# A selective-scan block with experts on one core: the first scan group's products written straight into the result tile, the skip term added by a DMA of half the size

## The chip, the cores and the metric

The kernel runs on one core of a Trainium2 chip. The metric is the device time of one execution in microseconds, as the median of several runs. Five engines work side by side, each through its own list of instructions in order: TensorE (PE, with its weight loads as PEld), VectorE (DVE), ScalarE (ACT), GpSimd (POOL) and SyncE (SP, which here only issues transfers). POOL issues transfers too: those that add into their destination.

## The reference, cut to what matters

The input `x` is 16 samples of 256 positions with 256 features. Each sample is normalised; two branches are computed from the normalised sample and added to `x`.

```python
xn = layernorm(x)
# branch 1, per sample: E = 512 features, N = 16 states
hidden, gate = split(einsum('blh,he->bel', xn, W_in))
hidden = silu(causal_conv4(hidden) + conv_bias)
dt, Bm, Cm = split(hidden^T @ W_x, [128, 144])
dts = softplus(dt @ W_dt + b_dt)
dA  = exp(dts * A);  dBu = dts * Bm * hidden
state_t = dA_t * state_(t-1) + dBu_t            # scan over positions
scan_out = sum over the 16 states of state * Cm
y = (scan_out + hidden * D) * silu(gate)        # hidden * D is the skip term
branch1 = y^T @ W_out
# branch 2: 32 experts of width 96, the 8 best per position
branch2 = sum_e weight_e * (silu(xn @ w_gate_e) * (xn @ w_up_e)) @ w_down_e
out = x + branch1 + branch2
```

Everything is float32.

## The kernel before, in words

The work of one sample `b` is a set of small steps, each of one engine (the functions named below). They are not written in order. A planner (`Plan`, L20) is given for each step its engine, an assumed length, the steps it needs, the buffers it takes and gives back, and a due time: a base for the sample (`ORIGIN`, `PERIOD`, `RATE`) plus an offset for the kind of step (`DUE`, with `FIRST` and `LAST` for the first and last sample). It plays the engines through, always starting the ready step that is due first and prefers, by `STAY`, a step that needs no new activation table on ACT. The order that comes out is the order of the program. So a change of one step's length, needs or due time can move the steps of every engine, also of samples far apart. Buffers come in rings (`RINGS`): the n-th taker of a ring of size k waits until the (n-k)-th has been given back.

The scan branch of a sample:

- `load_x` (SP) loads `xt`; `stats`, `root`, `invert` give mean and deviation; `norm` (L366, ACT) writes the normalised sample into `xn`; `turn` (PE) transposes it into PSUM and `keep_turned` (ACT) copies it to `xnT`.
- `project` (PE, two halves, into PSUM banks "g" and "u"), `conv_first` (ACT) and `conv_rest` (DVE, twelve operations, L540) and `activate` (ACT) make `hs`. `params` (PE, `px`), `keep_params`, `send_params`, `widen`, `steps` make `dts`. `inputs` (L605, POOL) multiplies `dts` into `hs`, in place.
- The 16 states are taken in 8 groups `g` of two, and the four chunks of 128 features in two halves `u`; so there are 16 units per sample, each of two chunks. `fetch` (SP) brings the two B and C rows of a group to all partitions (`rep`). `feed` (POOL, L629) makes `bu` for a unit. `decay` (ACT, L643), `scan` (DVE, L651) and `read` (DVE, L661) run once per chunk; `read` multiplies the states with C and writes the products to `pr`, a ring of four.
- The sum over groups is made by transfers that add: `collect` (L664, issued by POOL) adds the 128 x 1024 products of a unit to `y[b, u]`. A `y` tile has two slots for the two states of a group. Before the first `collect` of a sample, `skip` (L594, ACT, one per chunk) has written hidden * D into slot 0 and `clear` (L601, POOL) zeros into slot 1. Collects of one `y` tile wait for each other's landing.
- After the last group `fold` (POOL, L685) adds the two slots, `gated` (POOL, L710) multiplies with the gate from `gate` (PE) and `gate_silu` (ACT), and `project_out` (PE, L720, `po`) multiplies with W_out. In the last sample DVE does the last collects and the gating.

The expert branch: `route` (PE, `pl`), `largest`, `expo`, `choose` (ten small DVE operations, L404 to L434) select and weigh the experts; `send_weights` writes the weights to DRAM (four transfers) and `spread` brings them to all partitions (`wr`, six transfers for a quarter). `gates` and `ups` (PE, L473, `pg` and `pu`), `silu` (ACT), `weigh` (POOL, L492), `combine` (DVE, L496, `h`) and `down` (PE, L508, `acc`) run over 12 pairs of chunks per sample.

The end of a sample: `load_again` (SP) loads `x` once more into `o`, `settle` and `finish` (DVE) add `acc` and `po` to it, and `store` (SP) writes it out. `o` is a ring of two.

At the start SP also loads all the weights: the experts' weights in four parts.

Of the kernel before, what the change touches and what calls it, by code (L numbers as in the profile page):

```python
# [11 lines left out]
F32 = mybir.dt.float32  # L12
AF = mybir.ActivationFunctionType
ALU = mybir.AluOpType
# [5 lines left out]
class Plan:  # L20
# [10 lines left out]
    STAY = -18.3  # L31
# [89 lines left out]
def mamba_moe_kernel(  # L121
# [30 lines left out]
    nc = tc.nc  # L152
# [26 lines left out]
    ORIGIN = -1.8  # L179
    PERIOD = 79.7  # L180
    RATE = 80.2

    DUE = dict(
        load_x=-146.0, stats=-45.5, root=-39.5, invert=-189.5, norm=235.5, turn=-297.0,
        keep_turned=-116.5, route=-81.5, largest=-193.5, expo=-102.5, choose=-538.5,
        send_weights=-21.0, project=-77.5, conv_first=328.0, conv_rest=265.5, activate=-374.5,
        params=-132.0, keep_params=-109.5, send_params=-242.0, widen=-104.5, steps=-17.0,
        skip=149.0, clear=-5.5, inputs=-96.5, fetch=-122.5, feed=168.5, decay=-16.5, scan=322.5,
        read=-130.1, collect=-20.0, spread=42.0, gates=-33.5, ups=238.5, silu=300.0, weigh=-19.5,
        combine=-120.0, down=26.5, settle=-222.0, gate=49.5, gate_silu=-159.0, fold=129.0,  # L190
        gated=378.5, project_out=-121.5, load_again=8.0, finish=-12.5,
    )
    EARLY = dict(
        load_x=171.0, load_experts=55.0, stats=31.0, turn=155.0, route=63.0, project=243.0,
# [3 lines left out]
        route=-144.0, largest=-26.0, expo=57.5, choose=266.0, project=309.5, conv_first=-246.5,  # L198
        conv_rest=-160.5, activate=289.0, params=-357.5, keep_params=261.5, widen=-38.5,
        steps=574.5, skip=-263.0, clear=-16.0, inputs=125.0, fetch=4.0, feed=-148.5, decay=-125.5,  # L200
        scan=-243.0, read=-43.0, collect=-97.5, spread=-33.5, gates=-12.5, ups=-178.5, silu=-161.0,
        weigh=288.0, combine=344.0, down=57.0,
# [3 lines left out]
        fetch=5.5, feed=-85.5, decay=55.5, scan=369.0, read=-177.5, collect=-114.5, spread=-3.5,  # L206
        gates=372.0, ups=44.5, silu=146.0, weigh=51.0, combine=141.5, down=275.5, settle=-6.0,
        gate=-31.5, gate_silu=-75.5, fold=-120.5, gated=412.0, project_out=-172.0, finish=299.5,
    )
    LEAD = -9.2  # L210
# [13 lines left out]
        xt=1, mv=1, st=1, std=1, xn=1, xnT=3, nmax=1, rest=1, dt=1, hs=2, dts=2, y0=2, y1=2,  # L224
        rep=3, bu=3, pr=4, da=AHEAD, g=2, u=2, acc=1, wr=2, sg=3, h=2, gs=2, o=2,
# [140 lines left out]
    def norm(b):  # L366
        xt = live["xt", b]
        rstd, nmr = live.pop(("st", b))
        xn = p1.tile([P, SPS, H], F32, tag="xn", name=f"xn_{b}")
        for s in range(SPS):  # L370
            nc.scalar.activation(
                xn[:, s, :], xt[:, s, :], AF.Identity, bias=nmr[:, s, :], scale=rstd[:, s, :]
            )
        live["xn", b] = xn

    def turn(b):
        xn = live.pop(("xn", b))
        pt = bank(f"pt_{b}", "u")
        for hc in range(HC):
            for s in range(SPS):  # L380
                nc.tensor.transpose(pt[:, ts(hc * SPS + s, P)], xn[:, s, ts(hc, P)], ident)
        live["pt", b] = pt
# [211 lines left out]
    def skip(b, c):  # L594
        hs = live["hs", b]
        u, j = divmod(c, CPU)
        if j == 0:
            live["y", b, u] = take(sb, f"y{u}", [P, CPU, NG, L], f"y_{b}_{u}")
        nc.scalar.activation(live["y", b, u][:, j, 0, :], hs[:, c, :], AF.Copy, scale=dsk[:, c, :])

    def clear(b):  # L601
        for u in range(PAIRED):
            nc.gpsimd.memset(live["y", b, u][:, :, 1, :], 0.0)
# [52 lines left out]
    def read(m):  # L656
        k, j = divmod(m, CPU)
        b, g, u = unit(k)
        if j == 0:
            live["pr", k] = take(sb, "pr", [P, CPU, NG, L], f"pr_{b}_{g}_{u}")  # L660
        nc.vector.tensor_mul(live["pr", k][:, j], live.pop(("da", m)), live["rep", b, g][:, 1])  # L661
# [86 lines left out]
    def add(kind, key, engine, length, due, *args, early=None, **kw):  # L748
# [15 lines left out]
        clear=clear, fold=fold, send_params=send_params, send_weights=send_weights, collect=collect, decay=decay, scan=scan, read=read,  # L764
# [17 lines left out]
    for b in range(B):  # L782
# [11 lines left out]
        add("norm", (b,), "ACT", 1.09, t, b, needs=[("invert", b)], takes=[("xn", ("xn", b))],  # L794
            gives=[x, ("rs", b)])
        xT = ("xnT", b)
        add("turn", (b,), "PE", 1.0, t, b, needs=[("norm", b)], gives=[("xn", b)],
# [33 lines left out]
        for c in range(EC):  # L831
            u, j = divmod(c, CPU)
            add("skip", (b, c), "ACT", 0.42, t, b, c,
                needs=[("activate", b)] + ([("skip", b, c - 1)] if j else []),
                takes=[] if j else [(f"y{u}", ("y", b, u))], gives=[hs])
        add("clear", (b,), "POOL", 0.93, t, b, needs=[("skip", b, c) for c in range(EC)])
# [7 lines left out]
        for r in range(UNITS):  # L844
# [5 lines left out]
            for j in range(CPU):  # L850
# [8 lines left out]
                    takes=[] if j else [("pr", ("pr", k))], gives=[("da", m), ("rep", b, g)])  # L859
            reads = [("read", CPU * k + j) for j in range(CPU)]  # L860
            if b == B - 1 and g == GROUPS - 1:
                add("collect", (k,), "DVE", 1.25, at + PERIOD / SLOTS, k, fn=collect_last,
                    needs=reads + [("fold", b, u)], gives=[("pr", k)])
                continue
            add("collect", (k,), "POOL", 0.61, at + PERIOD / SLOTS, k,
                needs=reads + [("clear", b)] + ([("collect", k - PAIRED)] if g else []),
# [88 lines left out]
```

## Time and profile before

| | us |
|---|---|
| median of 3 runs (1335.29 to 1336.34) | 1335.97 |
| the profiled execution, its own time | 1333.77 |
| its span, first to last instruction | 1332.0 |
| PE busy (97% of the span) | 1290.4 |
| POOL busy (89%) | 1189.2 |
| DVE busy (88%) | 1174.2 |
| ACT busy (86%) | 1142.6 |

The profile's times are those of one execution; a span is a little shorter than the time of the execution, and the sums below are made against the profiled execution. Rows of an engine name the source line, the operation and the tiles (result, then sources). The bracket behind a timeline row is the time for which the engine stood idle ahead of it, with the work whose end released it. One matmul step of the program is eight instructions of PE in such a row ("x8"), since a float32 matmul runs as two. The busy time of POOL contains time in which an operation is listed while the issue of a transfer ahead of it still holds the engine, so POOL's own cost is better read from one start to the next.

### The profile page before, as it was taken

How to read it: one execution, taken by the hardware profiler on the slowest of the kernel's cores; microseconds unless marked ns; L12 is line 12 of the kernel's file. 1: busy time of each engine (PE TensorE's matmuls, PEld its weight loads, DVE VectorE, ACT ScalarE, POOL GpSimd, SP SyncE). 2: the span in 40 equal slices, each digit the busy share in tenths (PEclk: the TensorE clock that was granted, in tenths of full speed). 3: DMA queues.
4: the chain of work that ended last, by engine and by line, in shares of the span. 5: the costliest groups of instructions: out<-in, count | busy, mean ns of one | idle time of the engine just before them, and what ended most of it. 6: DMA issues, size and time to landing. Idle time of an engine off the chain costs nothing.

```text
span 1332.0 us, 18939 instructions
## 1 busy us (share of the span) xinstructions
PE 1290.4 (97%) x5968; PEld 1109.9 (83%) x5968; DVE 1174.2 (88%) x1735; ACT 1142.6 (86%) x1904; POOL 1189.2 (89%) x835
## 2 busy tenths in 40 slices
PE   8979989999999999999999999999999999999998
PEld 6858778888888888888888888888888888888777
DVE  3878998989899898988989899798989989899896
ACT  5878698898989979799897988979899898987873
POOL 1769989999898999989899998999999999899995
PEclk9989999999999999999999999999999999999999
DMA  9999899899999899999999999989998998989994
GB/s 250 260 227 216 190 234 213 188 216 206 213 201 214 203 206 218 191 216 204 204 218 191 215 207 207 216 194 216 199 224 187 210 230 194 212 200 221 209 213 94
DMA packets 169941, 277.19 MB, mean 208 GB/s; under 512 B 37840, under 2 KB 103920, under 8 KB 169840
## 3 DMA queue, kind: packets, MB, share of 16 engines
q0 software_dynamic: 36576, 133.19, 53.1%
q1 hardware_dynamic: 130624, 142.75, 38.5%
q8 instruction: 47, 0.77, 0.2%
q10 hardware_dynamic: 2640, 0.05, 0.1%
q14 instruction: 54, 0.44, 0.1%
HBM read 137.51 MB, written 5.24 MB: 107 GB/s over the span
## 4 chain that ended last, share of the span: by engine, by line
PE 44%; DVE 17%; POOL 13%; issue 9%; DMA 8%; ACT 8%; SPq 1%; ACTq 0%; POOLq 0%; DVEq 0%
PE acc L508 11%; PE pg L473 10%; PE pu L473 10%; DVE da L651 6%; DMA rep<-bcd 5%; POOL bu L629 5%; POOL sg L492 5%; PE po L720 4%; PE px L555 4%; DVE hs L540 4%; DVE pr L661 4%; ACT da L643 3%; POOL y L666 2%; DMA y<-pr 2%; PE ph L519 2%
## 5 line engine op out<-in xcount | busy, mean ns | idle before, releaser
L629 POOL TENSOR_TENSOR bu<-rep,hs 128x1024 f32<-128x1024 f32 x256 | 726.7, 2942 | 73.3 <-DVE da L651 34.7
L651 DVE TENSOR_TENSOR_SCAN da<-da,bu 128x512 f32<-128x512 f32 x512 | 607.3, 1216 | 36.0 <-ACT da L643 26.0
L643 ACT ACTIVATE da<-dts,a_sb 128x256 f32<-128x256 f32 x1024 | 470.6, 473 | 90.9 <-DVE pr L661 68.9
L473 PE MATMUL pu<-xnT,wu_sb 128*128 128x256 f32 x1536 | 360.0, 381 | 12.3 <-DVE h L496 12.0
L508 PE MATMUL acc<-wd_sb,h 128*128 128x256 f32 x1536 | 363.4, 380 | 0.3 <-DVE o L732 0.3
L666 POOL DMA_DIRECT2D y<-pr x254 | 349.1, 1378 | 14.5 <-DVE h L496 5.2
L473 PE MATMUL pg<-xnT,wg_sb 128*128 128x256 f32 x1536 | 352.0, 383 | 9.2 <-ACT sg L486 7.0
L661 DVE TENSOR_TENSOR pr<-da,rep 128x512 f32<-128x512 f32 x512 | 336.1, 676 | 3.2 <-issue 1.6
L473 PEld LDWEIGHTS pu<-xnT,wu_sb 128*128 128x128 f32 x1536 | 292.3, 191 | 54.8 <-DVE h L496 14.4
L473 PEld LDWEIGHTS pg<-xnT,wg_sb 128*128 128x128 f32 x1536 | 294.5, 192 | 51.4 <-ACT sg L486 8.2
L508 PEld LDWEIGHTS acc<-wd_sb,h 128*128 128x128 f32 x1536 | 291.6, 191 | 39.9 <-DVE o L732 0.6
L492 POOL TENSOR_TENSOR sg<-sg,wr 128x512 f32<-128x512 f32 x192 | 295.6, 1793 | 32.4 <-ACT rstd L353 24.9
L496 DVE TENSOR_TENSOR h<-pu,sg 128x512 f32<-128x512 f32 x192 | 131.3, 684 | 81.7 <-POOL sg L492 39.9
L643 ACT ACT_TABLE_LOAD x154 | 197.6, 1283 | 2.8
L486 ACT ACT_TABLE_LOAD x81 | 103.9, 1283 | 1.5
L486 ACT ACTIVATE sg<-pg 128x512 f32<-128x512 f32 x192 | 104.0, 593 | 0.9
L540 DVE SCALAR_TENSOR_TENSOR hs<-ph,small,hs 128x255 f32<-128x255 f32 (+2 forms) x192 | 90.2, 478 | 5.3 <-ACT hs L531 0.7
L710 POOL TENSOR_TENSOR y<-y,gs 128x512 f32<-128x512 f32 x30 | 73.8, 2893 | 0.1
L685 POOL TENSOR_TENSOR y<-y 128x512 f32<-128x512 f32 x32 | 71.3, 2230 | 0.0
L720 PE MATMUL po<-wout_sb,y 128*128 128x256 f32 x256 | 61.6, 384 | 9.9 <-DVE hs L540 7.8
L720 PEld LDWEIGHTS po<-wout_sb,y 128*128 128x128 f32 x256 | 47.4, 190 | 21.0 <-POOL y L710 7.8
L555 PE MATMUL px<-hs,wx_sb 128*32 128x256 f32 (+1 forms) x256 | 61.4, 387 | 2.4 <-ACT sg L486 2.4
(64 smaller groups left out, 804.3 us busy)
## 6 DMA issues: line engine op xcount, KB each, us to landing
y<-pr POOLq DMA_DIRECT2D x254, 512.0 KB, 7.0
rep<-bcd SPq DMA_DIRECT2D x128, 512.0 KB, 6.4
wr<-wd SPq DMA_DIRECT2D x128, 192.0 KB, 6.2
wr<-wd SPq DMA_DIRECT2D x128, 128.0 KB, 6.1
wr<-wd SPq DMA_DIRECT2D x128, 64.0 KB, 5.7
xt<-L_attn_input_states_dram SPq DMA_DIRECT2D x16, 256.0 KB, 6.9
o<-L_attn_input_states_dram SPq DMA_DIRECT2D x16, 256.0 KB, 6.0
out_dram<-o SPq DMA_DIRECT2D x16, 256.0 KB, 5.2
```

What stands on the lines that cost most here:

```text
L473: nc.tensor.matmul(p[:, j, :], w[:, hc, ts(c, P)], xs[:, hc, :], start=(hc == 0), stop=(hc == HC - 1),)
L486: nc.scalar.activation(sg, live.pop(("g", b, q)), AF.Silu)
L492: nc.gpsimd.tensor_mul(sg, sg, wr[:, r : r + 2, :])
L496: nc.vector.tensor_mul(h, live.pop(("u", b, q)), live.pop(("sg", b, q)))
L508: nc.tensor.matmul(acc[:, s, :], h[:, j, ts(s, P)], wd_sb[:, c, :], start=(c == 0 and s == 0), stop=(c == FC - 1), skip_group_check=True,)
L540: nc.vector.scalar_tensor_tensor(cv[:, c, k:], ph[:, j, : L - k], cw[:, c, KC - 1 - k : KC - k], cv[:, c, k:], op0=ALU.mult, op1=ALU.add,)
L629: nc.gpsimd.tensor_mul(bu, live["rep", b, g][:, 0:1].to_broadcast([P, CPU, NG, L]), live["hs", b][:, ts(u, CPU), :].unsqueeze(2).to_broadc ...
L643: nc.scalar.activation(da[:, i, :], dts[:, c, :], AF.Exp, scale=a_sb[:, c, n : n + 1])
L651: nc.vector.tensor_tensor_scan(flat, flat, live["bu", k][:, j].rearrange("p n l -> p (n l)"), 0.0, op0=ALU.mult, op1=ALU.add,)
L661: nc.vector.tensor_mul(live["pr", k][:, j], live.pop(("da", m)), live["rep", b, g][:, 1])
L666: nc.gpsimd.dma_start(live["y", b, u].rearrange("p c n l -> p (c n l)"), live.pop(("pr", k)).rearrange("p c n l -> p (c n l)"), accum_op=A ...
L720: nc.tensor.matmul(po[:, s, :], y[:, j, 0, ts(s, P)], wout_sb[:, c, :], start=(c == 0 and s == 0), stop=(c == EC - 1), skip_group_check=True,)
```

## The change

Five things are done.

1. The first group's `read` writes its products straight into the new `y` tile, which stands for `pr` in that unit. The products of group 0 are no longer collected.
2. `skip` writes to a tile of its own, `sk` (one buffer), and not into `y`. For group 0 a new step `add_skip` stands in the place of `collect`: a transfer, issued by POOL, that adds half a sample's `sk` (256 KB instead of 512) into slot 0 of `y[b, u]`.
3. `clear` with its two memsets per sample is gone.
4. `norm` writes the normalised sample over `xt`; the tile `xn` is gone, and `xt` is given back by `turn` instead of `norm`.
5. `o` has one buffer instead of two, and the planner's due times and its other constants have other values.

```diff
-    STAY = -18.3
+    STAY = -28.0
...
-    ORIGIN = -1.8
+    ORIGIN = -3.0
     PERIOD = 79.7
-    RATE = 80.2
+    RATE = 79.8
...
-    LEAD = -9.2
+    LEAD = -8.0
...
-        xt=1, mv=1, st=1, std=1, xn=1, xnT=3, nmax=1, rest=1, dt=1, hs=2, dts=2, y0=2, y1=2,
-        rep=3, bu=3, pr=4, da=AHEAD, g=2, u=2, acc=1, wr=2, sg=3, h=2, gs=2, o=2,
+        sk=1, xt=1, mv=1, st=1, std=1, xnT=3, nmax=1, rest=1, dt=1, hs=2, dts=2, y0=2, y1=2,
+        rep=3, bu=3, pr=4, da=AHEAD, g=2, u=2, acc=1, wr=2, sg=3, h=2, gs=2, o=1,
...
-        xn = p1.tile([P, SPS, H], F32, tag="xn", name=f"xn_{b}")
         for s in range(SPS):
             nc.scalar.activation(
-                xn[:, s, :], xt[:, s, :], AF.Identity, bias=nmr[:, s, :], scale=rstd[:, s, :]
-            )
-        live["xn", b] = xn
+                xt[:, s, :], xt[:, s, :], AF.Identity, bias=nmr[:, s, :], scale=rstd[:, s, :]
+            )
...
     def skip(b, c):
         hs = live["hs", b]
-        u, j = divmod(c, CPU)
-        if j == 0:
-            live["y", b, u] = take(sb, f"y{u}", [P, CPU, NG, L], f"y_{b}_{u}")
-        nc.scalar.activation(live["y", b, u][:, j, 0, :], hs[:, c, :], AF.Copy, scale=dsk[:, c, :])
-
-    def clear(b):
-        for u in range(PAIRED):
-            nc.gpsimd.memset(live["y", b, u][:, :, 1, :], 0.0)
+        if c == 0:
+            live["sk", b] = take(sb, "sk", [P, EC, L], f"sk_{b}")
+        nc.scalar.activation(live["sk", b][:, c, :], hs[:, c, :], AF.Copy, scale=dsk[:, c, :])
+
+    def add_skip(b, u):
+        nc.gpsimd.dma_start(
+            live["y", b, u][:, :, 0, :], live["sk", b][:, ts(u, CPU), :], accum_op=ALU.add
+        )
...
     def read(m):
         k, j = divmod(m, CPU)
         b, g, u = unit(k)
-        if j == 0:
+        if j == 0 and g == 0:
+            live["y", b, u] = live["pr", k] = take(sb, f"y{u}", [P, CPU, NG, L], f"y_{b}_{u}")
+        elif j == 0:
             live["pr", k] = take(sb, "pr", [P, CPU, NG, L], f"pr_{b}_{g}_{u}")
...
+            if g == 0:
+                add("collect", (k,), "POOL", 0.61, at + PERIOD / SLOTS, b, u, fn=add_skip,
+                    needs=reads, gives=[("sk", b)], lands=6.5)
+                continue
             add("collect", (k,), "POOL", 0.61, at + PERIOD / SLOTS, k,
-                needs=reads + [("clear", b)] + ([("collect", k - PAIRED)] if g else []),
+                needs=reads + [("collect", k - PAIRED)],
                 gives=[("pr", k)], lands=7.8)
```

All values of `DUE`, `EARLY`, `FIRST` and `LAST` differ too. The order of the instructions that the planner makes of them, engine by engine in both builds, is what the prediction calls the old and the new order. On PE the number and size of the steps are the same in both; DVE has the same operations; POOL issues 254 transfers before and 254 after, 32 of them of the new kind, and 32 memsets less; on ACT the passes are the same and the table loads are fewer.

## The prediction

> **What bounds the kernel now.** I read the stages first (busy time in stretches of 80 us, one sample each), then TensorE's own waits, then the timeline at each of its gaps, then POOL and the queues.
>
> Stretches; columns are the length, then busy time with instruction counts of PE, weight loads, DVE, ACT and POOL, then the granted clock, the DMA share and GB/s:
>
> ```profile
> core 0: us, PE busy (x) PEld busy (x) DVE busy (x) ACT busy (x) POOL busy (x), PEclk, DMA share, GB/s
> 20.00:100.00 80.00, 67.38 (x298) 55.48 (x297) 55.34 (x86) 67.67 (x110) 50.70 (x33) 0.94 0.96 246
> 180.00:260.00 80.00, 75.85 (x343) 64.83 (x342) 73.14 (x107) 69.04 (x119) 73.24 (x53) 0.96 0.91 207
> 660.00:740.00 80.00, 79.22 (x372) 68.48 (x371) 72.25 (x109) 71.17 (x120) 74.18 (x53) 1.00 0.94 205
> 900.00:980.00 80.00, 80.00 (x377) 69.27 (x376) 73.45 (x109) 72.12 (x122) 74.99 (x53) 1.00 0.94 210
> ```
>
> From 900 to 1140 us PE is never idle: TensorE is the bound, and no other engine is above 75 of 80. In the longest chain the same `acc` step starts at 904.57, 984.02, 1063.55 and 1143.01, so a sample costs 79.48 us there. Before that the `po` steps start at 482.03, 562.38, 643.10, 723.46 and 804.08: 80.5 us. PE's waits from 260 to 1220 us explain the difference (us in total, times, longest):
>
> ```profile
> PE po L720 <- DVE hs L540: 7.8, 9, 1.5
> PE pu L473 <- DVE h L496: 0.6, 1, 0.6
> ```
>
> The first matmuls of `project_out` wait, once a sample, for the last `conv_rest` on DVE: `po` takes the "u" bank that `project` filled. The other gaps lie at the start and the end. Timeline of PE (start, length, in brackets the idle time before):
>
> ```profile
> 82.13 3.78 PE L473 MATMUL pu<-xnT,wu_sb 128*128 128x256 f32 x8 [6.87 <-DVE h L496]
> 155.53 1.89 PE L473 MATMUL pg<-xnT,wg_sb 128*128 128x256 f32 x8
> 159.66 3.62 PE L473 MATMUL pg<-xnT,wg_sb 128*128 128x256 f32 x8 [2.24 <-DVE hs L540]
> 180.83 3.62 PE L473 MATMUL pg<-xnT,wg_sb 128*128 128x256 f32 x16
> 195.15 6.38 PE L473 MATMUL pg<-xnT,wg_sb 128*128 128x256 f32 x16 [3.80 <-ACT sg L486]
> 643.10 1.97 PE L720 MATMUL po<-wout_sb,y 128*128 128x256 f32 x8 [1.13 <-DVE hs L540]
> 1257.17 3.72 PE L473 MATMUL pg<-xnT,wg_sb 128*128 128x256 f32 x16 [1.97 <-ACT sg L486]
> ```
>
> All idle gaps of PE add up to 42 us (1332.0 less 1290.4 busy): 4.6 before 25 us, some 20 from 56 to 276, 7.8 at `po`, 5.7 after 1250, the rest where the span begins and ends. What the change can win lies in these. After the larger gaps the matmuls are slow too: 8 take 3.62 instead of 1.89, 16 take 6.38 instead of 3.62.
>
> **The change part by part.** It consists of work taken off POOL, ACT and the queues, and of an order that comes out different on every engine.
>
> POOL. Start to start, a copy with adding holds it for 0.61 us and the two memsets of a sample for 0.94:
>
> ```profile
> 601.08 0.88 POOL L666 DMA_DIRECT2D y<-pr  x1
> 601.69 2.80 POOL L492 TENSOR_TENSOR sg<-sg,wr 128x512 f32<-128x512 f32 x2
> 655.81 1.59 POOL L603 MEMSET y<- 128x512 f32 x2
> 656.75 1.52 POOL L666 DMA_DIRECT2D y<-pr  x1
> ```
>
> A sample has 16 feeds (2.30 each, start to start), 12 weighings (1.23), 16 copies (0.61), 4 passes of fold and gating (1.24), `inputs` (2.5) and the memsets (0.94): 36.8+14.8+9.8+5.0+2.5+0.9 = 69.8 of 79.5 us. The memsets go: -0.94. The two copies of group 0 become two skip copies, each 256 pieces of 1 KB instead of 128 of 4 KB; no row has that shape. Below, 0.61 as the nearest row (issuing half the bytes is not cheaper than that row shows); above, 1.22, if the cost follows the pieces. I take 0.8: +0.4 a sample. POOL gains some 0.5 us a sample (-0.9 to +0.3), covered by PE's 79.5: worth 0. Were that cover gone, 16 samples would make -8 us.
>
> Queues. The `y<-pr` queue takes 53.1% of 1332 us for 254 copies, 2.78 us of all engines each; half the bytes save 1.4, 32 times, 44 us of queue time. No PE gap of the middle waits for a transfer: 0. The next copy onto the same `y` half waits for the skip copy's landing (7.0 us is the median of a full one); five to six POOL steps, 8 us, stand between them: 0, at most 1 us a sample of POOL's slack of 9. Tightest is a pair of later copies onto one half, 5.8 us apart in the new order: some 1.2 us of waiting, with the last feed, `inputs` and the weighings 10 and 11 behind it; their products are due about 7 us later. 0.
>
> `norm` in place and one `o` buffer. ACT's two passes per sample are the same (587 ns each); the next load of `xt` stands behind the transposes in both kernels. With one `o` buffer, `load_again` waits for the store (5.2 us to land), and `fetch` of the next group 0 is queued behind it on SP. Between store and load SP now has `bcd`, a `rep` and the four `wd` writes, which `route`, moved up, has put there; today the four take 3.2 us and the load follows the store after 5.3 even without them. The store has landed: 0, at most 2 us on a `rep` that is needed some 20 us later.
>
> ACT. Its order has 13 table loads fewer (142 for `decay` instead of 154, 31 for the steps instead of 32): 13 x 1.283 = 16.7 us. ACT is at 71 of 80: 0.
>
> The wait at `po`, which is where the time is. In the old order `route` stands directly before `project`, so the ten small operations of `choose` (713.86 to 715.75 in that sample) stand on DVE ahead of the twelve of `conv_rest`; between `ph_1` and `po` PE has 4 steps, 6.9 us, and conv is 1 us late. In the new order `route` follows `params` of the sample before, `choose` is out of the way (2 us), and one more `acc` step (1.73) stands before `po`: conv then ends 2.5 us early. Late next are the "g" bank that `choose` must free before `pg_10` (1.6 us to spare by counting rows) and `h_2` before its `acc` (0.9, the same distance as today). So the waits go: -7.8.
>
> The start. The new order reaches its repeating form on PE with sample 2, the old one with sample 4. The gaps at 159.66 and 195.15 belong to the irregular part: 2.24+3.80 idle, and 1.73+2.76 of slow matmuls, 10.5 us. Here the Trainium skill speaks: "TensorE: Matmul & The Clock Gate", section "What's actually happening", halves the clock after an idle window of about 3.4 us. By it the gap of 2.24 would cost only itself and the sum at stake would be 8.8; the row shows the halving after 2.24 (and none after 1.97), so I use 10.5. But those gaps only partly come from the order: POOL starts its feeds at 41.5, stands 9.46 us for `rep` until 74.6, and is the late one until about 194 (`inputs` of sample 2 there, 155 us after that of sample 0, for 124 us of work). The change takes 1.6 us from this stretch of POOL and puts other loads ahead: six `wr` transfers before the first `rep`, so feeds start some 2 us later (inside the 9.46). By bytes at 252 GB/s (18.5 MB until 74.5 us) `rep_3`, with 0.77 MB less before it, lands at 71.4, and `rep_4` at 79.8; the weighing for `h_6` is now behind the feed that needs `rep_4`: 82.7 instead of 79.80. The gap of 6.87 grows by 2.6 to 3, the ones near 160 and 195 shrink. Ends: -10.5 if both gaps go and nothing grows, +5 if none goes. I take -2, near the POOL row, as it is the engine that is late there.
>
> The end: 5.7 us of gaps now; the new order interleaves `acc` more and puts the last gate projection just before the last two `acc` steps. 0 (-3 to +3).
>
> Sum: -7.8 - 2.0 = -9.8. The profiled execution took 1333.77, its span is 1332.0; 1333.8 - 9.8 = 1324.0. The median of the runs is 2.2 above the profiled one: 1326.
>
> **The rivals.** *Everything irregular goes.* The start loses its 10.5 and the end 3: 1336 - 7.8 - 10.5 - 3 = 1315, with half of it 1318. For: the early repeating order. Against: the 9.46 us for `rep`, which nothing removes. 0.16.
>
> *The change does not do what it says.* Memsets and bytes are hidden anyway, and the 1 us at `po` comes back at `pg_10` or in an `acc` step, whose margins are 0.9 to 1.6 us: 1336. For: those margins. Against: samples 11 to 13 of today already run without a gap. 0.10.
>
> *Slower: weighing behind `rep_4`.* Place: POOL at about 80 us. Each us that `rep_4` lands after 79.8 delays `h_6` and PE as much, and the lag is carried on. At the 225 GB/s of the stretch 40 to 190 us it lands at 88: gap 6.87 + 2.6 + 8 = 17.5, that is +10.6, with 3 us more of slow clock; less 7.8: 1342. From a landing at about 84.5 it decides. For: DMA share of 0.96 here. Against: the bytes ahead of it are known. 0.24.
>
> **How the numbers follow.** Forecast 0.50, with 1321 to 1333 as its own range. Within 0.2% (2.7 us) a measurement of this kernel can't be told from no change. Faster: 0.50 + 0.16 = 0.66; same 0.10; slower 0.24. The range leaves out about a third of the good rival (below 1316) and half of the slower one (above 1342): 1316 to 1342.
>
> **What would show it.** Right: PE at 80.00 of 80 from sample 3 on, `po <- hs` gone from PE's waits, `acc` steps 79.5 us apart throughout, no memset row, the skip copies at most 1.2 us each. Wrong: a new wait of PE in every sample; a gap above 10 us near 82; POOL waiting for `y<-pr` more than 5 us a sample.

## The result, and the profile after

| | before | changed |
|---|---|---|
| median, us (4 runs each) | 1336.15 (1335.29 to 1339.57) | 1377.74 (1371.84 to 1378.26) |
| span of the profiled execution | 1332.0 | 1370.1 |
| PE busy / idle in it | 1290.4 / 41.6 | 1306.8 / 63.3 |

The changed kernel is slower: ratio 1.0296, 95% interval 1.0263 to 1.0329. The forecast was 1326 us with a range of 1316 to 1342. The medians differ by 41.6 us, the spans of the profiled executions by 38.1. The table's last row splits the 38.1: 21.7 us more in which PE stands, and 16.4 us more in which the same 5968 matmuls are listed as busy.

The stretches of 80 us again (columns as in the prediction):

```profile
20.00:100.00 80.00, 69.79 (x300) 57.13 (x300) 55.48 (x92) 67.59 (x110) 53.76 (x35) 0.94 0.91 234
180.00:260.00 80.00, 76.24 (x345) 64.78 (x343) 67.64 (x100) 65.07 (x107) 68.96 (x49) 0.98 0.81 185
660.00:740.00 80.00, 77.36 (x353) 65.70 (x352) 71.57 (x107) 67.30 (x112) 69.51 (x50) 0.98 0.85 190
900.00:980.00 80.00, 79.46 (x370) 67.71 (x369) 73.54 (x111) 70.81 (x120) 73.44 (x52) 1.00 0.92 204
```

The first row is no worse than before (69.79 us of PE instead of 67.38). The third holds 353 matmuls instead of 372, at a clock of 0.98 instead of 1.00, and *every* other engine does less too (POOL 69.51 instead of 74.18). So no engine became the bound by its work: all wait for each other. PE's waits over the whole run show for what (us in total, times, longest):

```profile
PE acc L506 <- DVE h L494: 26.1, 18, 3.4
PE pu L471 <- DVE h L494: 14.5, 7, 4.0
```

The first line is new. It is the sign that the prediction named for its own failure, a new wait of PE: eight of the 18 waits are long, 2.2 to 3.4 us, one in each of the samples 2 to 9; the other ten are 0.2 to 0.4 us. Of the `pu` waits four, of 1.9 to 2.2 us, lie in the last samples. The `po` waits on `conv_rest` (7.8 us) are no longer listed; on PE's timeline they are under 0.2 us each. From the start of one sample's first `po` step to the next, worked out from PE's timeline, in us:

| kernel | samples 1 to 2, 2 to 3, ... |
|---|---|
| before | 78.1, 79.0, 81.1, 80.7, 80.4, 80.7, 80.4, 80.6, 80.5, 79.4, 79.5, 79.5, 79.8, 93.8, 27.7 |
| changed | 85.6, 85.4, 85.7, 84.9, 85.8, 85.0, 84.5, 86.0, 80.8, 82.6, 81.6, 81.5, 79.8, 78.0, 27.7 |

Eight samples lose about 5 us each, 41.9 us together; that is the whole loss (the entries behind them sum to 8.2 us less than before, and the first `po` starts 3.4 us later). The later ones, where the planner's order is another, run at 81.5. (`po` stands at another place of the sample in the old order, so the last entries compare only as sums.)

Now backwards from one of these waits. PE, timeline of the changed kernel:

```profile
713.02 2.55 PE L506 MATMUL acc<-wd_sb,h 128*128 128x256 f32 x8 [2.16 <-DVE h L494]
715.37 4.79 PE L695 MATMUL pgate<-xnT,win_sb 128*128 128x256 f32 x16
```

The gap costs 2.16 us, and the matmuls behind it are slow: 2.55 and 4.79 us instead of 1.89 and 3.62, 1.8 us more. This `acc` belongs to pair 10, the last but one of the sample's pairs 0 to 11. Its `h` (`h_10` below) waits for the weighing on POOL:

```profile
702.95 2.35 POOL L628 TENSOR_TENSOR bu<-rep,hs 128x1024 f32<-128x1024 f32 x1 [7.28 <-DMA rep<-bcd]
708.19 2.61 POOL L607 TENSOR_TENSOR hs<-dts,hs 128x1024 f32<-128x1024 f32 x1
710.98 2.50 POOL L490 TENSOR_TENSOR sg<-sg,wr 128x512 f32<-128x512 f32 x2
```

The weighings (710.98) stand behind `inputs` (708.19), and that behind the two feeds of group 7, the first of which stood 7.28 us for its `rep`. That `rep` was issued late, by SP:

```profile
667.36 14.59 SPq L616 DMA_DIRECT2D rep<-bcd  x2
682.05 0.41 SPq L240 DMA_DIRECT2D xt<-L_attn_input_states_dram  x1
684.45 4.72 SPq L457 DMA_DIRECT2D wr<-wd  x6
689.27 1.19 SPq L741 DMA_DIRECT2D out_dram<-o  x1
690.56 0.45 SPq L569 DMA_DIRECT2D bcd<-bc  x1
694.09 0.38 SPq L616 DMA_DIRECT2D rep<-bcd  x1
```

Between the seventh fetch (the second of the first row) and the eighth (694.09) stand `xt`, six `wr` transfers, the store and `bcd`. Its own buffer was free at 689.4. After `bcd` it waited 3.1 us more, and SP's waits say for what:

```profile
SPq L616 <- DMA wr<-wd: 24.7, 8, 3.6
```

In the traces SP's transfers signal their completion on eight counters that are used in turn, and an issue waits until the transfer that used its counter last has landed. The eighth fetch comes eight transfers after the first of the `wr` six, which landed at 694.03: 24.7 us, 8 times, in just the eight samples of 85 us. In the old order only `bcd` and the load of `o` stand between the two fetches; `xt` and the six are behind.

### The profile page after: what moved, and what is told of

It is laid out like the page before. It is cut to its first block, busy times and chain, and to the rows that moved or that the text cites. A ratio compares the mean times of both kernels' runs of the same rounds, so it can differ in the third digit from the quotient of the medians.

```text
span 1370.1 us, 18834 instructions
## 1 busy us (share of the span) xinstructions
PE 1306.8 (95%) x5968; PEld 1115.7 (81%) x5968; DVE 1178.3 (86%) x1735; ACT 1124.8 (82%) x1891; POOL 1182.9 (86%) x803
## 5 line engine op out<-in xcount | busy, mean ns | idle before, releaser
L628 POOL TENSOR_TENSOR bu<-rep,hs 128x1024 f32<-128x1024 f32 x256 | 788.0, 3473 | 113.4 <-DMA rep<-bcd 46.9
L506 PE MATMUL acc<-wd_sb,h 128*128 128x256 f32 x1536 | 376.0, 389 | 26.1 <-DVE h L494 26.1
L490 POOL TENSOR_TENSOR sg<-sg,wr 128x512 f32<-128x512 f32 x192 | 351.8, 2386 | 31.8 <-DMA wr<-wd 25.8
L506 PEld LDWEIGHTS acc<-wd_sb,h 128*128 128x128 f32 x1536 | 296.9, 194 | 75.2 <-DVE h L494 33.8
L471 PE MATMUL pg<-xnT,wg_sb 128*128 128x256 f32 x1536 | 347.9, 379 | 1.3 <-DVE hs L538 1.1
L471 PEld LDWEIGHTS pg<-xnT,wg_sb 128*128 128x128 f32 x1536 | 291.6, 190 | 41.9 <-issue 1.4
L662 DVE TENSOR_TENSOR pr<-da,rep 128x512 f32<-128x512 f32 x448 | 293.6, 677 | 1.7
L494 DVE TENSOR_TENSOR h<-pu,sg 128x512 f32<-128x512 f32 x192 | 130.7, 681 | 103.4 <-POOL sg L490 81.6
L686 POOL TENSOR_TENSOR y<-y 128x512 f32<-128x512 f32 x32 | 89.8, 3153 | 3.1 <-DMA y<-pr 3.1
L600 POOL DMA_DIRECT2D y<-sk x32 | 76.5, 2390 | 0.1
L517 PE MATMUL ph<-xnT,win_sb 128*128 128x256 f32 x256 | 62.9, 391 | 2.5 <-ACT sg L484 2.5
```

What stands on the lines that cost most here:

```text
L471: nc.tensor.matmul(p[:, j, :], w[:, hc, ts(c, P)], xs[:, hc, :], start=(hc == 0), stop=(hc == HC - 1),)
L490: nc.gpsimd.tensor_mul(sg, sg, wr[:, r : r + 2, :])
L494: nc.vector.tensor_mul(h, live.pop(("u", b, q)), live.pop(("sg", b, q)))
L506: nc.tensor.matmul(acc[:, s, :], h[:, j, ts(s, P)], wd_sb[:, c, :], start=(c == 0 and s == 0), stop=(c == FC - 1), skip_group_check=True,)
L628: nc.gpsimd.tensor_mul(bu, live["rep", b, g][:, 0:1].to_broadcast([P, CPU, NG, L]), live["hs", b][:, ts(u, CPU), :].unsqueeze(2).to_broadc ...
L686: nc.gpsimd.tensor_add(y[:, :, 0, :], y[:, :, 0, :], y[:, :, 1, :])
```

## The experiments

Ratios are against the kernel before, timed beside each changed one. My theory 1 was that the order causes the loss, at the place just shown; theory 2 that the new half-size transfer does; theory 3 that the single `o` buffer or the norm in place does.

**Operations against constants: x1, x2.** x1 (x2 the other way round):

```diff
-    STAY = -28.0
+    STAY = -18.3
...
-    LEAD = -8.0
+    LEAD = -9.2
```

and so for `ORIGIN`, `RATE`, `DUE`, `EARLY`, `FIRST` and `LAST`.

> The changed kernel (skip term by add_skip, no memsets, norm in place, one o buffer) with all of the planner's constants (STAY, ORIGIN, RATE, LEAD, DUE, EARLY, FIRST, LAST) set back to those of the kernel before, so that the planner makes another order. Theory 1 (the loss of 41.6 us is in the order that the new constants make: the eighth fetch of a sample comes late, bu of group 7 waits on POOL, and the last weighings wait behind it): 1325 to 1345 us, no wait of acc for h above 2 us in each sample. Theory 2 (the half-size transfer itself costs it, by its issue or its landing): 1365 to 1380 us. Theory 3 (the single o buffer or the norm in place costs it): 1365 to 1380 us too.

Measured: 1480.1 us, ratio 1.107 (1.1042 to 1.1099).

> The kernel before (skip written into y, memsets, xn, two o buffers) with the planner's constants of the changed kernel; the two constants of clear, which the changed kernel no longer has, stay as before. Theory 1 (the order): the loss comes along with the constants, 1360 to 1385 us. Theories 2 and 3 (the transfer; the buffers): no loss, 1330 to 1345 us.

Measured: 1447.3 us, ratio 1.0828 (1.0804 to 1.0852). No theory's numbers were near, in either. Each mix gives a third order, worse than both: here a set of constants is good only for the steps that it was made with. So this pair decides nothing, and the next one fixes the order itself.

**Operations against order: x6, x7.** The order of steps that one kernel's planner makes is written out as a list, and the other kernel's steps are issued by it:

```diff
-        for st in self.order():
+        by = {st["name"]: st for st in self.steps}
...
+        for name in ORDER:
...
+            if name in by:
+                steps.append(by[name])
...
+        for st in steps:
             st["fn"](*st["args"])
```

These are the lines of x6, cut. x6 has two `o` buffers, which the old order needs; in x7 `clear` stands just ahead of each sample's first `collect`.

> The changed kernel's operations (first products into y, sk and add_skip, no memsets, norm in place), issued in the order of steps that the planner of the kernel before makes, add_skip standing where the collect of group 0 stood; o has two buffers, since that order loads it again before it is stored. Theory 1 (the loss is in the order): 1322 to 1338 us, at or below the kernel before. Theories 2 and 3 (the transfer, the norm in place): 1360 us and more. A miss of both would be that sk or the landing of add_skip holds up this order.

> The operations of the kernel before (skip into y, two memsets, xn, two o buffers), issued in the order of steps that the planner of the changed kernel makes, clear standing just ahead of each sample's first collect. Theory 1: the loss comes with the order, 1365 to 1385 us, with acc waiting for h each sample and the eighth fetch waiting for a weight quarter. Theories 2 and 3: 1330 to 1345 us.

| | old order | new order |
|---|---|---|
| old operations | 1 | x7: 1389.8 us, 1.0391 (1.0356 to 1.0426) |
| new operations | x6: 1339.3 us, 1.0020 (1.0011 to 1.0030) | changed: 1.0296 (1.0263 to 1.0329) |

The loss goes with the order, in both rows. The new operations (in x6 without the single `o`) cost 0.2% in the old order and *gain* 0.9% in the new one (1.0391 to 1.0296). x7 has the same two waits as the changed kernel; PE's and SP's waits of x7:

```profile
PE acc L523 <- DVE h L511: 28.1, 18, 3.9
```

```profile
SPq L632 <- DMA wr<-wd: 24.2, 8, 3.3
```

x6 was a small miss for theory 1, which allowed it to be faster than before: the old order keeps its own wait of `po`, and it is no smaller (PE's waits of x6; before 7.8 in 9):

```profile
PE po L738 <- DVE hs L555: 12.0, 9, 1.7
```

**The place in the order: x4, x9, x13.** Each moves transfers on SP from ahead of the eighth fetch to just behind it; the other engines keep their order. For x9 (cut):

```diff
...
+        for b in range(15):
+            at = {st["name"]: i for i, st in enumerate(steps)}
+            i, k = at["spread", b + 1, 0], at["fetch", b, 7]
+            if at["fetch", b, 6] < i < k:
+                steps[i : k + 1] = steps[i + 1 : k + 1] + [steps[i]]
...
```

x13 has `("send_params", b + 1)` in the place of `("spread", b + 1, 0)`. x4 moves all that SP issues between the two fetches (at `i` and `k`):

```diff
...
+            late = [st for st in steps[i + 1 : k] if st["engine"] == "SP"]
+            rest = [st for st in steps[i + 1 : k] if st["engine"] != "SP"]
+            steps[i + 1 : k + 1] = rest + [steps[k]] + late
```

> The changed kernel with one edit of SP's order: everything that SP issues between a sample's seventh and eighth fetch (the load of xt, the spread of a weight quarter, the store, the parameters) is moved behind the eighth fetch. The other engines keep their order. Theory 1: the eighth rows are issued some 5 us earlier, the wait of bu of group 7 falls from 7.3 us to below 3, the wait of acc for h (2.4 to 3.4 us, and some 2 us of slow clock behind it) is gone in samples 2 to 9, and the kernel gains 4 to 5 us in each of these eight: 1335 to 1350 us. Theories 2 and 3: within 5 us of the changed kernel, 1372 to 1382 us.

Measured: 1348.5 us, 1.0090 (1.0069 to 1.0111). As theory 1 had it; theories 2 and 3 missed by 23 us and more.

> The changed kernel with one step per sample moved on SP: the six transfers of the next sample's first weight quarter (spread) stand behind the eighth fetch in the eight samples in which they stood ahead of it; the load of xt, the store and the parameters keep their place ahead of it. If those six transfers (4.7 us of issue, and the completion of the first, for which the eighth fetch waits 3.1 us) are the whole delay: as good as the move of everything (1348.5 us) or better, 1330 to 1350 us, periods of 79.5 to 82 us in samples 2 to 9. If store and load are needed for it too: 1355 to 1370 us.

Measured: 1341.6 us, 1.0047 (1.0030 to 1.0064). Six transfers in each of eight samples, moved in one queue from ahead of the fetch to just behind it, give back most of the 41.6 us: 36 us by the medians, 33 by the ratios. That is more than x4 gives, which moves `xt`, the store and `bcd` as well. The periods of samples 2 to 9 are 80.5 to 82.1. SP, POOL and PE in x9, at the same place of a sample whose `ph` starts at 558.02 (in the changed kernel above, at 664.81):

```profile
583.47 0.36 SPq L622 DMA_DIRECT2D rep<-bcd  x1
583.92 4.54 SPq L463 DMA_DIRECT2D wr<-wd  x6
```

```profile
591.40 2.35 POOL L634 TENSOR_TENSOR bu<-rep,hs 128x1024 f32<-128x1024 f32 x1 [1.76 <-DMA rep<-bcd]
```

```profile
604.73 1.89 PE L512 MATMUL acc<-wd_sb,h 128*128 128x256 f32 x8
```

The fetch goes out 25.5 us after `ph` instead of 29.3, and POOL waits 1.76 us instead of 7.28. The `acc` of pair 10 starts without a wait, where it waited 2.16 us, and at full speed; so it is in all of the eight samples. The ten short waits of `acc` in x9 (3.2 us in all) are those of pair 9, which the changed kernel has too.

> The changed kernel with one transfer per sample moved on SP: the parameters (bcd, 0.45 us of issue) stand behind the eighth fetch in the eight samples in which they stood ahead of it. The eight completions of SP's transfers are used in turn, so the eighth fetch then stands for its completion behind the load of xt and no longer behind the first transfer of the weight quarter; the six transfers themselves stay ahead. If the wait for that completion (24.7 us in 8 places) is the larger part of the loss: the fetch is issued 3 us earlier in eight samples, 1345 to 1358 us. If the issue of the six is the larger part: 1360 to 1372 us.

Measured: 1361.3 us, 1.0175 (1.0150 to 1.0199). By its number that is the second case, but the wait for the counter only went from the fetch to the transfer that took its place (waits of SP in x13):

```profile
SPq L622 <- DMA bcd<-bc: 34.4, 8, 5.3
SPq L575 <- DMA wr<-wd: 24.3, 8, 3.3
```

`bcd` now waits for the `wr`, and the next sample's first fetch 4.3 us for `bcd`. So the time alone does not split the loss. The traces do, as far as the rows of the eighth fetch go. From the issue of `xt`, mean of the samples 2 to 9, in us:

| kernel | fetch issued | its rows landed | POOL's wait for them |
|---|---|---|---|
| changed | 12.0 | 21.4 | 7.9 |
| x13: the six ahead, no wait of the fetch for the counter | 8.3 | 19.6 | 6.1 |
| x9: the six behind | 7.3 | 15.1 | 1.8 |

POOL in x13, at the same place:

```profile
692.21 2.34 POOL L634 TENSOR_TENSOR bu<-rep,hs 128x1024 f32<-128x1024 f32 x1 [5.48 <-DMA rep<-bcd]
```

In x13 the fetch is issued 3.7 us earlier than in the changed kernel, but its rows land only 1.8 us earlier. Putting the six behind it brings another 4.5 us. So the smaller part of the delay is the wait for the counter; the larger is that the fetch takes longer to land with the six ahead of it (11.4 us from its issue in x13, 7.8 in x9). How PE's loss splits between the two is not shown.

**The transfer: x3, x5.** Both kernels leave the skip term out of the result.

```diff
     def add_skip(b, u):
-        nc.gpsimd.dma_start(
-            live["y", b, u][:, :, 0, :], live["sk", b][:, ts(u, CPU), :], accum_op=ALU.add
-        )
+        return                                    # x3
+        sk = live["sk", b]                        # x5, without the return
+        nc.gpsimd.memset(sk[:, ts(u, CPU), :], 0.0)
+        nc.gpsimd.memset(sk[:, CPU * u, :], 0.0)
```

> The changed kernel with the transfer of add_skip left out (the skip term is missing from the output); the order of all other work is the same. Theory 1: within 5 us of the changed kernel, 1372 to 1382 us. Theory 2 (the transfer costs it by its issue of 0.8 us, two per sample, or by the bandwidth and landing of 256 KB): at least 15 us faster, 1335 to 1360 us. Theory 3: 1372 to 1382 us.

Measured: 1327.4 us, 0.9930 (0.9903 to 0.9956). Against my theory 1, and what theory 2 asks for: without the two transfers per sample the kernel is 50 us faster, with the six `wr` still ahead of the fetch. Its periods tell how: 85.4, 79.4, 85.0, and then 79.3 to 79.5 nine times. The slow period is there at the start and then lets go, and PE is never idle again (stretch of x3, against the third row of the changed kernel):

```profile
660.00:740.00 80.00, 80.00 (x377) 69.46 (x376) 73.58 (x109) 70.79 (x120) 72.28 (x49) 1.00 0.86 197
```

> The changed kernel with add_skip's transfer replaced by two memsets of POOL on the half of sk that it would have read (the skip term is missing from the output): about 0.75 us of POOL per add_skip as with the transfer (0.74 to 0.78 from start to start), but no bytes moved and no landing to wait for. Leaving the transfer out altogether gave 1327.4 us. If POOL's time for the issue is what tips it: 1360 to 1380 us. If the transfer's landing or its traffic is: 1322 to 1335 us.

Measured: 1362.2 us, 1.0191 (1.0166 to 1.0217). With bytes and landing gone, 15.6 of the 50 us are won, and the eight samples stay at 83.8 to 85.6. The memsets take 1.7 us of POOL per sample, the two transfers 2.4 (each from the end of the operation ahead to its own end; the part on why the prediction was wrong says why it is read so). So x5 does not quite keep POOL's time, as was meant, but it differs from x3 in its memsets alone, and their 1.7 us make 34.8 us. So it is mainly POOL's time that tips it, in a kernel in which POOL stands idle 10 us a sample; whether the other 15.6 us come from the remaining 0.7 us of POOL or from the bytes and the landing is not shown. Theories 1 and 2 are then both in part right. As I read it, there is a chain through all engines, from `ph` over the convolution, the fetches, POOL and `h_10` back to PE, that is longer than PE's 79.4 us of work. The six transfers lengthen it at one place, POOL's issues at another; taking away either brings it near PE's own period, and the two gains (36 and 50 us) cannot be added. One link that closes it shows in the traces: the first of the six waits for POOL's weighing 8 (which ended at 684.42; issue at 684.45, 19.6 us after `ph`). In the samples 5 to 9 of x3 that issue comes 17.6 us after `ph`, and the rows of the eighth fetch land after 33 us instead of 38 to 40, though the six are still ahead.

**The buffer: x12.**

```diff
-        ... gs=2, o=1,
+        ... gs=2, o=2,
-    plan = Plan(RINGS)
+    plan = Plan(dict(RINGS, o=1))
```

> The changed kernel with two buffers for o and the order of all steps kept (planned as for one). Theory 3, or my own estimate that a single o costs up to 2 us where a fetch stands behind load_again: SP waits 7.0 us in 5 places for the store before it may load again, and the first fetches of the next sample stand behind. If that matters: 1365 to 1373 us. If not, as the order theory has it: 1375 to 1380 us.

Measured: 1375.4 us, 1.0301 (1.0272 to 1.0330), the changed kernel's 1.0296 again. The single `o` costs nothing, and with it half of theory 3 falls. The norm in place was not tried alone, but is among the operations of x6.

**Looking for a faster version: x8, x10, x11.** All three move a step on POOL *back*, to let another go first. The step at `i` goes behind the one at `k`:

```diff
...
+            i, k = at["inputs", b + 1], at["weigh", b, 11]              # x8, on x4
+            i, k = at["collect", 16 * b + 11], at["feed", 16 * b + 15]  # x10, on x4
+            i, k = at["collect", 16 * b + 12], at["weigh", b, 11]       # x11, on x9, late samples
+            if i < k:
+                steps[i : k + 1] = steps[i + 1 : k + 1] + [steps[i]]
```

> The changed kernel with the eighth fetch moved ahead on SP as before (1348.5 us by itself), and on POOL the product inputs of the next sample moved behind the last two weighings. Theory 1: the last h of a sample comes 2.7 us earlier, what acc and pu still wait for h is gone, 1330 to 1342 us. If what is left of the loss lies elsewhere (decays and feeds of the next sample wait for inputs): 1345 to 1355 us.

> The kernel that moved everything behind the eighth fetch (1348.5 us) with one more edit on POOL: the collect that stands just ahead of the last feed of a sample is moved behind that feed. In the trace of 1348.5 us it waits 1.8 us for the landing of an older collect in 9 places (14.1 us in all), with the last feed, inputs and the last two weighings behind it. If that wait holds up inputs: 1335 to 1344 us. If the scan then only waits for pr instead (the collect is later, and frees it later): 1345 to 1355 us.

> The move of the six transfers alone, and in samples 10 to 15, whose order is another one (there the period of the changed kernel is 81.5 us and the eighth fetch does not wait for a weight quarter), the collect that stands ahead of inputs moved behind the last two weighings. Against the move of the six transfers alone: 1 to 2 us less in each of six samples, 6 to 12 us in all, if that collect's wait holds up inputs and with it the last h (pu waits 1.9 to 2.2 us for it); within 3 us if not.

Measured: 1371.8 (1.0262; 1.0232 to 1.0291), 1368.3 (1.0244; 1.0218 to 1.0269) and 1370.6 us (1.0257; 1.0227 to 1.0286). All three lie outside every case that was expected, 13 to 26 us above the slower one. What looked like a queue with the urgent step at its end behaves like a chain in which each step is urgent. In x11 POOL waits 33.9 us in 12 places for the landing of an older collect, where x9 has 14.8 in 9, and the late samples went from 81 to 87 us, with the wait of x7 back (PE's waits of x11, 3.2 in 10 in x9):

```profile
PE acc L517 <- DVE h L505: 23.0, 16, 4.5
```

**The rest: x14, x15, x16.** The step at `k` goes ahead to `i`, each kernel with the edits of the one before, x14 on x9; x16 moves what lies between its two steps and is a `decay` behind the second:

```diff
...
+            i, k = at["scan", 32 * b + 10], at["combine", b, 2]  # x14, DVE, four late samples
+            i, k = at["skip", b, 2], at["skip", b, 3]            # x15, ACT, right behind i
+            i, k = at["steps", b, 0], at["steps", b, 1]          # x16, ACT
```

> The move of the six transfers alone (1341.6 us) with one edit on DVE: in the four late samples in which the third h of a sample stands behind a scan that waits 3.4 us for bu, it is moved ahead of that scan. Its operands are there before the scan starts, and the scan waits for bu in any case. If pu's wait for that h (1.2 to 2.1 us in four places, two of them with 1.7 us of slow clock behind it) is what is left of the loss there: 9 to 14 us less, 1327 to 1333 us, below the kernel before. If something else is late at the same place: 1338 to 1344 us.

Measured: 1341.4 us, 1.0026 (1.0015 to 1.0038). By the medians nothing, by the ratios some 3 us with intervals that overlap, not the 9 to 14 expected. The gap that was aimed at is closed, and the period is still 81.5 us, one stretch like the next (x14, stretches of one period):

```profile
980.00:1061.50 81.50, 80.42 (x373) 68.47 (x373) 73.87 (x109) 70.16 (x118) 74.19 (x53) 1.00 0.89 198
1061.50:1143.00 81.50, 80.41 (x373) 68.47 (x373) 73.86 (x109) 70.17 (x118) 74.19 (x53) 1.00 0.89 198
```

A wait of PE that I took away came back as smaller ones elsewhere. What was left to shorten stood on POOL (waits of x14 from 980 to 1143 us):

```profile
POOL hs L618 <- ACT sk L607: 4.9, 2, 2.5
```

> x14 (the six transfers behind the eighth fetch, the h ahead of its scan; 1341.4 us) with the fourth skip of every sample moved on ACT right behind the third. If the wait of inputs for that skip (2.5 us in each of the late samples) sets their period: inputs and the last weighings come up to 2.5 us earlier, the period falls from 81.5 to 79.5 or 80 us in four to five samples, 1331 to 1336 us. If inputs then waits for another thing or nothing follows from it: 1339 to 1344 us.

Measured: 1337.6 us, 1.0013 (1.0003 to 1.0024). The late samples fall to 80.6 to 81.3, the gain is 2 to 4 us, again with intervals that overlap: in the right direction, less than expected.

> x15 with one more edit on ACT: the decay that stands between the two softplus steps of a sample is moved behind the second, so that the table is switched twice less (2.6 us of ACT per sample, in a stretch in which DVE's scan waits for the decays behind it and inputs for the skip). If ACT's chain from the convolution to inputs sets the period of 81 us in the early samples and 81.5 in the late ones: 79.4 to 80 us each, 1322 to 1332 us. If not: within 3 us of x15.

Measured: 1338.4 us, 1.0013 (1.0000 to 1.0026): nothing. So the changed operations can be brought level with the kernel before, within 0.2%, by three small moves of order; nothing that computes everything was faster than it. What holds x15 at 80.7 us, where x3 reaches 79.4, stays open.

## Why the prediction was wrong, by its own steps

- *What bounds the kernel* held: PE, with 79.4 us of work per sample (x3 runs at it), and the loss is waits of PE with slow matmuls behind most of them.
- *Queues*, the step that failed. The working followed on SP only `load_again` and the fetch behind it, and put every transfer of the middle at 0. It did not list what the new order puts ahead of the *eighth* fetch: `xt`, six `wr`, the store. With the six ahead, the rows of that fetch land 6.3 us later after `xt` in eight samples (21.4 against 15.1 in x9), and their place makes 33 to 36 us.
- The same part named the victims, "the last feed, `inputs` and the weighings 10 and 11", and called their products due 7 us later. That margin was counted from rows and is mis-sized: with the fault repaired, `h_10` ends 0.1 to 1.2 us ahead of its `acc` in x9, and 1.5 to 1.8 us ahead in the samples 5 to 9 of x3. In the changed kernel it comes 2.2 to 3.4 us too late. In one sample of each, the eighth fetch goes out about as late after `ph` in the old order as in the new (30.2 and 29.3 us); but the old order weighs pairs 10 and 11 at 52.4 us after `ph`, the new at 46.2. The lateness is not the fetch's alone, it is that its consumer was moved 6 us ahead.
- *POOL*: the price of a skip copy was too low. From start to start it is 0.74 to 0.79 us in nearly every place, as taken. But behind issues the operations of POOL are listed as longer than they are by themselves, and an engine that needs their result waits for the end that is listed. A weighing, which takes 1.26 us where nothing was issued ahead of it, ended 3.75 us after its start, and DVE stood idle for just that end (656.83 + 3.75 = 660.58):

```profile
656.83 3.75 POOL L490 TENSOR_TENSOR sg<-sg,wr 128x512 f32<-128x512 f32 x1
660.62 0.69 DVE L494 TENSOR_TENSOR h<-pu,sg 128x512 f32<-128x512 f32 x1 [3.28 <-POOL sg L490]
```

  So, against what is said ahead of the prediction, POOL's time is better read from one end to the next:

```profile
723.96 2.35 POOL L667 DMA_DIRECT2D y<-pr  x2
725.08 2.46 POOL L600 DMA_DIRECT2D y<-sk  x1
```

  The collects end at 726.31, the skip copy at 727.54: 1.23 us, and 1.15 for the other of the sample, near the upper figure of the prediction (1.22). A collect takes 0.8 to 0.9 in this way, the two old memsets 0.92 a sample. So the change saves POOL some 0.2 us a sample and not 0.5, and its slack before was 5 us (75 of 80 busy in the prediction's own stretch) and not 9. "Covered by PE's 79.5: worth 0" was wrong too: x5 against x3 makes 1.7 us of POOL per sample worth 34.8 us. An average slack covers nothing when the work stands in a chain. The row of the skip copies on the changed kernel's page is no price either, since its 2390 ns contain the issues ahead, and half the bytes land hardly sooner:

```profile
L600 POOL DMA_DIRECT2D y<-sk x32 | 76.5, 2390 | 0.1
```

```profile
y<-pr POOLq DMA_DIRECT2D x222, 512.0 KB, 8.0
y<-sk POOLq DMA_DIRECT2D x32, 256.0 KB, 7.4
```

- *The wait at `po`*, -7.8: right that `choose` is out of the way, wrong in size. In the changed kernel 0.14 to 0.18 us a sample are left, and in its relatives the wait is back at about 0.5 us (x9: 4.1 us in 8, x15: 5.5 in 11; before 7.8 in 9). In all of these `po` starts 0.26 us after the convolution's end, as before, so the convolution does not end 2.5 us early. It comes near that only in x3, where it ends 2.0 us ahead of `po` in most samples.
- *The start*, -2: the gap near 82 us shrank, from 6.87 to 4.03 us; but the first `po`, which stands at another place of its sample, is not earlier (166.6, before 163.2), so nothing of the 2 us can be shown. The rival "weighing behind `rep_4`" did not occur; the kernel is slower by the same kind of wait, at the eighth `rep` and once per sample, where the rival had it once, at the fifth.
- *Norm, `o`, ACT* at 0: right for `o` (x12); no run tries the norm or the 13 table loads alone.
- The working had no case in which a small delay repeats in each sample. The counter's wait alone, 3.1 us in eight samples, would have been 25 us, and with the 5 us per sample that were lost the range would have had to reach to 1376.

## What to carry to other kernels

When an order changes, list for every queue what now stands ahead of each transfer that an engine waits for, once per repeating period; a few us there are multiplied by the number of samples. Where all engines are 85 to 95% busy and each waits a little for another, as here, do not take an engine's slack for cover: price an edit by whether it lies on the chain that sets the period, not by the busy share of its engine. Where issues of transfers stand among operations, read an engine's time from end to end, since that is what the others wait for. Constants tuned for one set of steps said nothing about another: to separate operations from order, carry the finished order over.

## What the runs showed of the hardware that I had not expected

The first is what decides on the slow clock after a gap of PE. The prediction read one halving after 2.24 us and none after 1.97 as an edge. By the length of the gap there is no edge. From 95 to 1250 us of sixteen of the traces (all but x1 and x2), a granted clock below 0.9 in the 8 us from the end of a gap followed

| gap, us | 0.9-1.5 | 1.5-1.9 | 1.9-2.3 | 2.3-2.6 | 2.6-3.0 | 3.0-5.0 |
|---|---|---|---|---|---|---|
| slow, of all | 0 of 49 | 1 of 35 | 8 of 23 | 10 of 20 | 10 of 12 | 25 of 33 |

Where it followed, those 8 us mostly read 0.79: 1.7 us lost. A gap of 2 us so costs 2 us or 3.7; none below 1.5 us cost more than itself.

What decides is where the gap lies. In the clock records of all the traces the granted clock is 1.0 or 0.5, and it changes only on a grid of 3.413 us. Here are two gaps of the changed kernel of nearly the same length, 2.16 us (from 710.86) and 2.19 us (from 986.40), in windows of that grid (columns as in the stretches):

```profile
710.90:714.31 3.41, 1.29 (x6) 1.16 (x7) 2.03 (x3) 1.67 (x3) 3.40 (x5) 1.00 0.15 53
714.31:717.73 3.42, 3.42 (x10) 2.67 (x9) 3.42 (x6) 2.27 (x5) 3.42 (x3) 0.50 0.89 196
```

```profile
983.95:987.37 3.42, 2.45 (x12) 1.81 (x10) 0.65 (x1) 1.51 (x2) 3.42 (x5) 1.00 1.04 206
987.37:990.78 3.41, 2.19 (x10) 1.96 (x11) 3.41 (x6) 2.12 (x3) 3.41 (x4) 1.00 1.03 257
990.78:994.19 3.41, 3.41 (x18) 3.00 (x17) 2.08 (x4) 2.54 (x7) 3.41 (x5) 1.00 0.77 161
```

The first gap lies in one window, in which PE stands for 2.12 us, and the next window runs at half the clock. The second is cut in two, 0.97 and 1.22 us, and no window is slow. By PE's idle time in one window at full clock, over the same sixteen traces:

| idle in the window, us | below 1.5 | 1.5-1.85 | 1.85-2.0 | 2.0-3.4 |
|---|---|---|---|---|
| next window slow, of all | 0 of 5266 | 0 of 28 | 4 of 13 | 48 of 48 |

So there is an edge, between 1.85 and 2.0 us of idle time within one window. For the program it is still chance, since the grid starts at another place in each trace. The Trainium skill ("TensorE: Matmul & The Clock Gate", section "What's actually happening") has the window, 3413 ns long and not tied to the start of the kernel, and the traces agree. Its idle window of about 3.4 us, which the prediction cited, need not be idle from end to end: some 2.0 us of it were enough. The measurement decides, and the prediction was right to set that figure aside, though not to put a length of gap in its place.

The second is the coupling itself: two different edits, of six transfers on one queue (x9) and of two transfers that take 2.4 us of another engine (x3), each moved the whole kernel from a period of 85 us to one near PE's own, and in x3 both periods occur in one execution of one program.
